# A row recurrence on one core: the order of the instructions in its loop written anew

## The chip, the cores and the metric

The kernel runs on one core of a Trainium2 chip. The metric is the time of one execution on the device, in microseconds (us), as the median of several executions. Five engines of the core take part, each with its own instruction stream that it works through strictly in order: PE (TensorE, matrix products; its weight loads are shown apart as PEld), ACT (ScalarE), DVE (VectorE), POOL (GpSimd) and SP (SyncE, which here only issues transfers). Across engines, an instruction waits on semaphores for the results that it needs.

## The reference

The input `x` holds 8 images of 96 channels and 128 rows of 128 pixels, in float32. It is normalised in 32 groups of channels; a masked convolution along the row gives four gates for every pixel; and then the rows are run through one after the other, as an LSTM whose hidden state `h` is itself convolved along the row (three taps):

```
its = conv(groupnorm(x), W_is * mask) + b_is          # 1x3, along a row
def step((h, c), row_in):                             # one row of all images
    gates = conv1d(h, W_ss, 3 taps) + b_ss + row_in
    f, i, o = sigmoid(three of the gates);  g = tanh(the fourth)
    c_new = f * c + i * g
    h_new = o * tanh(c_new)
out = x + all h_new
```

Row r + 1 can't start before `h` of row r is there. So 128 rows follow each other.

## The kernel before

**Half-steps.** The 8 images are cut into two halves of 4, which know nothing of each other. A half-step `n` is one row of one half: row `n // 2`, half `n % 2`. There are 256. While one half's gates go through the pointwise work, TensorE has the other half's products. Rows are loaded in blocks of four, by transfers that SP issues.

**Even and odd pixels.** A row is held as even and odd pixels apart, and the three taps are worked out from sums and differences of neighbours. From `h` of a half, VectorE makes the operand `vs` (the sum, `total`, L600), then `vf` (the difference, `difference`, L604), and GpSimd makes `vd` (`shifted`, L608). The first products of the half's next row need `vs`, the following `vf`, later ones `vd`. In the text that follows, "vs" at L600 is the operand on which the next row of that half hangs.

**The pointwise chain of a half-step.** ScalarE copies one half of a bank (`cpA`, `cpB`, `cpC`, L526); VectorE makes the even and the odd pixels' gates from it (`lo`, L530, and `hi`, L534); ScalarE takes tanh (`ta`, L538) and sigmoid (`si`, L550). Then, for the even pixels (`a`) and the odd ones (`b`) apart:

- the gated product i * g: `gtb` on VectorE (L564), `gta` on GpSimd (L562);
- the new cell: `ceb`, then `cea`, on VectorE (L574), which add f * c (`fg`, L555);
- tanh of the cell on ScalarE: `thb`, `tha` (L579);
- `h`: `oub`, `oua` on VectorE (L587), and straight behind them `vs` (L600) and `vf` (L604).

Behind them VectorE adds `h` to the row of `x` that goes out (`re`, L621, an instruction with both inputs in SBUF).

**GpSimd's other work.** Besides `vd` and `gta` GpSimd prepares the input of a later block of rows, spread over the half-steps. For one image of four rows, in three parts: `W1` normalises the own pixels into the buffer `xw` (L297, `xw<-xr`), `W2` adds neighbours (`add_pixels`, L314, `xs<-xw`, 256 elements in each of 128 partitions), `W3` subtracts them (`subtract_pixels`, L318, 512 elements). And it normalises channels that are shared (`U`, L297, `hx<-x`, in 32 partitions). In three half-steps of four that is one instruction of 512 or 384 elements; in those that follow the first row of a block it is two, one of 512 and a small one of 128 elements. The two halves take the first row one behind the other, so in every eight half-steps there are two such, which I call the heavy ones. GpSimd's first instruction behind the residual addition, `W1`, is held until that addition is done, and `vd` until `vf` is.

**What sets the order.** All four engines' streams are written by hand. The string `PERIOD` (L717) is read once for each half-step: each word is one or two instructions; a mark behind it says of which half-step (`'` the one before, `+` the next, `*` the one after that). Each engine's stream is the sequence of its own words in it. `prepare` (L680) issues the words `W1` to `W3` and `U`.

Of the kernel before, what the change touches and what calls it, by code (L numbers as in the profile page):

```python
# [21 lines left out]
def kernel(  # L22
# [32 lines left out]
    nc = tc.nc  # L55
# [354 lines left out]
    def hold(made, until):  # L410
        if until.ins.engine != E.Pool:
            tc.add_manual_dep(
                made.ins,
                until.ins.name,
                mybir.DependencyInfo(
                    mybir.DependencyClass.Sync, mybir.DependencyReason.SCHED_ONLY
                ),
                reason="GpSimd starts when VectorE is done with both SBUF reads",
            )
# [5 lines left out]
    class HalfStep:  # L425
# [141 lines left out]
        def part(self, ap, lo, hi, t=None):  # L567
            ap = ap.rearrange("p (t b j) -> p t b j", t=2, b=BH)
            return ap[:, :, lo:hi] if t is None else ap[:, t, lo:hi]
# [95 lines left out]
    def work(n):  # L665
        if n < len(FIRST):
            return FIRST[n]
        row, s = divmod(n, NH)
        k, r = divmod(row, R)
        ahead, image = (k + 2, 0) if r == R - 1 else (k + 1, r + 1)  # L670
        return (
            shared(s, k + 1, *SHARED[r]) if k + 1 < NB else [],
            own(s, ahead, image) if ahead < NB else (),
            ([(load_rows, s, k + 2)] if r == R - 2 and k + 2 < NB else [])
            + ([LATER[n]] if n in LATER else []),
        )
# [3 lines left out]
    def prepare(n, which="123"):  # L680

        channels, image, rest = worked.setdefault(n, [list(parts) for parts in work(n)])
        now = []
        for name, engine in (("X", nc.scalar), ("U", nc.gpsimd)):
            if name in which:
                now += [part for part in channels if part[1] is engine]
                channels[:] = [part for part in channels if part[1] is not engine]
        for i in "123":
            if i in which and int(i) <= len(image) and image[int(i) - 1]:
                now.append(image[int(i) - 1])  # L690
                image[int(i) - 1] = None
        if image.count(None) == len(image) and n not in closed:
            closed.add(n)
            now += rest
        for part, *args in now:
            made = part(*args)
            if made is not None and made.ins.engine == E.Pool and residuals:
                hold(made, residuals[-1])
                residuals.clear()
# [3 lines left out]
    def finish(n):  # L703
        prepare(n)
        row, s = divmod(n, NH)
        k, r = divmod(row, R)
        if r == R - 1:
            store(s, k, R - 1 if k + 1 == NB else 0, R)
            if k + 2 < NB:
                load(s, k + 2)  # L710
        elif r == R - 2 and k + 1 == NB:
            store(s, k, 0, R - 1)
# [2 lines left out]


    PERIOD = (  # L717
        "1A hiC' D'' X siBb' 1B 2A siBa' 2B 0C' siA' 2A re'' 3C' taB' 1A 1B fg' W1 0C' 2B cpA 3C' "
        "2C loA cpB U W2 EC' 1C loB PB+ PA+ taCa' hiA 1C taCb' QA+ hiB gta' 2C siC' gtb' 3A 3B EA "
        "ceb' cpC EB cea' 0A thb' W3 loC 0B tha' PC+ oub' 0A oua' 3B 3A S' 0B QB* F' taA QC+"  # L720
    )
    PIXELS = {"a": (0, BH, 0), "b": (0, BH, 1)}
    SPLIT = ("taC", "siB", "gt", "ce", "th", "ou")
# [8 lines left out]
    def half_step(n):  # L732
        if n not in steps:
            steps[n] = HalfStep(n)
        return steps[n]

    def do(n, names, by_lanes=False):

        for name in names.split():
            if name in "UX":  # L740
                if n >= NH:
                    prepare(n - NH, name)
                continue
            if name[0] == "W":
                prepare(n - 1 + name.count("+") - name.count("'"), name.strip("W+'"))
                continue
            at = n
            for mark, offset in (("'", -1), ("+", 1), ("*", 2)):
                at += offset * name.count(mark)
                name = name.replace(mark, "")  # L750
            pixels = PIXELS[name[-1]] if name[:-1] in SPLIT and name[-1] in PIXELS else ()
            whole_name = name[:-1] if pixels else name
            tile_ = whole_name[-1] if whole_name[-1] in order else ""
            part = whole_name[: len(whole_name) - len(tile_)]

            if part in ("S", "F", "D"):
                at += NH
            if not 0 <= at <= last:
                continue
            step = half_step(at)  # L760
            if name in step.done or whole_name in step.done:
                continue
            if by_lanes and (part in OWN or part in H_PRODUCTS) and (
                at < last or part in ("P", "Q") or (part, order[tile_]) in step.halves
            ):
                if step.piece(part, order[tile_]):
                    step.done.add(name)
                continue
            step.done.add(name)
            getattr(step, PARTS[part])(*([order[tile_]] if tile_ else []), *pixels)  # L770
            if by_lanes and part == "re":
                finish(at)
# [44 lines left out]
    def begin():  # L817
        operands(0)
        do(0, "PA PB QA QB PC QC 1A 2A 1B 2B 1C 2C")
# [7 lines left out]
    def next_products():  # L827


        late[0:0] = [Scale(1, 0, BH - 1)]  # L830
        late.insert(1, Scale(1, BH - 1, BH, late[0].banks))
        for a in range(3):
            half_step(1).take_bank(a)
        do(2, "PA PB QA QB PC QC 1A 2A 1B 2B 1C 2C")
# [18 lines left out]
    def keep_warm(count):  # L853
# [13 lines left out]
        at(4, 13): lambda: shared_rows(nc.scalar, 0, 0, R),  # L867
        at(5, 8): begin,
        at(5, 9): lambda: do(0, "cpA cpB cpC"),
        at(5, 17): lambda: do(  # L870
            0, "loA hiA EA 0A 3A loB hiB EB 0B 3B loC hiC EC 0C 3C taA taB siB taC siC"
# [174 lines left out]
```

## Time and profile before

| what | value |
|---|---|
| time of three executions | 2034.54 to 2035.09 us, median 2034.84 us |
| the profiled execution, first to last instruction | 2036.7 us |
| mean clock granted to TensorE | 0.997 of full speed |
| busy: PE, PEld, DVE, ACT, POOL | 95%, 91%, 89%, 76%, 65% of the span |

The profiled execution's own time is given as its span; it lies 1.9 us, or 0.1%, over the median of the runs. Busy time of PE isn't the time that it is at its peak: its products are pipelined and run in two row groups of 64 side by side, and an instruction is drawn until its modelled end.

The profile names instructions by engine, line and tiles, as `POOL xs<-xw L314`. In the timeline a row has the start, the time that it lasted, the engine, the line, and in brackets the idle time just before it and what ended that. Where "x2" stands, two like instructions in a row are drawn as one, from the start of the first to the end of the second.

### The profile page before, as it was taken

What the parts mean: (1) busy time and instruction counts of PE and PEld (TensorE: products, weight loads), DVE (VectorE), ACT (ScalarE), POOL (GpSimd) and SP (SyncE); (2) the same over time, 40 slices, a digit from 0 to 9 for tenths busy, and PEclk for the clock granted to TensorE, in tenths of its full rate; (3) what the DMA queues carried; (4) which work ended last, traced back from release to release, by engine and by line L of the source; (5) the groups of instructions that cost most, each with busy time, mean ns of one, the idle gap of its engine ahead of it and who ended that gap; (6) DMA issues with size and microseconds to landing.
All of it is one profiled execution on the core that took longest, in us unless ns stands there. A gap on an engine that the chain in (4) does not pass through costs nothing.

```text
span 2036.7 us, 45537 instructions
## 1 busy us (share of the span) xinstructions
PE 1935.3 (95%) x16936; PEld 1847.4 (91%) x16936; DVE 1812.6 (89%) x3997; ACT 1555.9 (76%) x3417; POOL 1329.7 (65%) x1708
## 2 busy tenths in 40 slices
PE   0389999999999999999999999999999999999998
PEld 0279999999999999999999999999999999999997
DVE  5768999999999999999999999999999999999998
ACT  4777777777777777777777777777777777777776
POOL 3347766666666666667666666666666666676651
PEclk9989999999999999999999999999999999999999
DMA  9994343344333334433433443333344333434411
GB/s 381 423 313 115 75 107 94 94 115 115 94 79 100 94 94 115 115 94 79 99 95 93 115 115 97 79 97 102 89 113 115 100 83 90 106 90 106 115 32 32
DMA packets 103388, 237.16 MB, mean 116 GB/s; under 512 B 5952, under 2 KB 8896, under 8 KB 97280
## 3 DMA queue, kind: packets, MB, share of 16 engines
q1 hardware_dynamic: 103168, 234.25, 42.0%
q8 instruction: 135, 2.21, 0.5%
q14 instruction: 85, 0.70, 0.1%
HBM read 183.90 MB, written 50.33 MB: 115 GB/s over the span
## 4 chain that ended last, share of the span: by engine, by line
PE 82%; DVE 7%; POOL 5%; DMA 4%; issue 1%; ACT 1%; SPq 0%; POOLq 0%; DVEq 0%; ACTq 0%
PE ps L460 82%; DMA xs<-in_x_dram 4%; DVE x L621 2%; POOL hx L297 2%; POOL xw L297 1%; DVE bst L919 1%; POOL xs L314 1%; DVE hx L587 1%; POOL g L562 1%; DVE vs L600 1%; DVE c L574 1%; DVE ps L530 1%; DVE ps L534 1%; DVE vf L604 1%; PE ps L174 0%
## 5 line engine op out<-in xcount | busy, mean ns | idle before, releaser
L460 PE MATMUL ps<-vd,wl 64*128 64x256 f32 (+1 forms) x6096 | 1275.6, 381 | 0.8 <-DVE ps L534 0.2
L460 PEld LDWEIGHTS ps<-vd,wl 64*128 64x128 f32 (+1 forms) x6096 | 943.4, 186 | 29.9 <-issue 1.7
L460 PE MATMUL ps<-vf,wm 64*128 64x256 f32 (+1 forms) x3052 | 752.7, 381 | 0.2
L460 PE MATMUL ps<-vs,wm 64*128 64x256 f32 (+1 forms) x3052 | 703.3, 384 | 5.9 <-POOL vs L600 4.0
L538 ACT ACTIVATE g<-ps 32x256 f32<-32x256 f32 (+1 forms) x1021 | 468.5, 481 | 301.0 <-PE ps L460 294.4
L460 PE MATMUL ps<-xs,wx 64*128 64x256 f32 x3080 | 676.8, 377 | 11.1 <-POOL xs L314 11.1
L460 PEld LDWEIGHTS ps<-vf,wm 64*128 64x128 f32 (+1 forms) x3052 | 504.7, 186 | 13.5 <-issue 0.8
L460 PEld LDWEIGHTS ps<-xs,wx 64*128 64x128 f32 x3080 | 491.8, 187 | 18.9 <-POOL xs L314 11.6
L608 POOL TENSOR_TENSOR vd<-hx 128x512 f32<-128x512 f32 x257 | 266.7, 1038 | 351.2 <-DVE vf L604 343.0
L460 PEld LDWEIGHTS ps<-vs,wm 64*128 64x128 f32 (+1 forms) x3052 | 432.4, 187 | 38.2 <-DVE vs L600 24.2
L530 DVE TENSOR_TENSOR ps<-m,ps 128x256 f32<-128x256 f32 x768 | 325.8, 425 | 98.7 <-ACT m L526 81.7
L526 ACT ACTIVATE m<-ps,wl 128x256 f32<-128x256 f32 x766 | 360.7, 474 | 56.6 <-PE ps L460 32.2
L550 ACT ACTIVATE ps<-ps 96x512 f32<-96x512 f32 x767 | 388.7, 507 | 14.4
L460 PE MATMUL ps<-xs,wt 64*128 64x256 f32 x1530 | 384.6, 377 | 0.0
L621 DVE TENSOR_TENSOR x<-x,hx 96x512 f32<-96x512 f32 x254 | 371.1, 1461 | 0.0
L297 POOL TENSOR_SCALAR xw<-xr,rstd,nmr 128x512 f32<-128x512 f32 x252 | 205.8, 817 | 181.9 <-DVE x L621 174.9
L534 DVE TENSOR_TENSOR ps<-m,ps 128x256 f32<-128x256 f32 x768 | 301.1, 422 | 1.3 <-PE ps L460 1.2
L318 POOL TENSOR_TENSOR xs<-xw 128x512 f32<-128x512 f32 (+1 forms) x254 | 270.0, 1063 | 0.0
L460 PEld LDWEIGHTS ps<-xs,wt 64*128 64x128 f32 x1530 | 264.8, 187 | 1.5 <-issue 1.0
L574 DVE TENSOR_TENSOR c<-ps,g 96x256 f32<-96x256 f32 x508 | 207.1, 419 | 55.3 <-POOL g L562 36.0
L297 POOL TENSOR_SCALAR hx<-x,rstd,nmr 32x512 f32<-32x512 f32 (+2 forms) x309 | 222.8, 721 | 32.6 <-DVE x L621 2.2
L579 ACT ACTIVATE th<-c 96x256 f32<-96x256 f32 (+1 forms) x510 | 203.7, 412 | 49.7 <-DVE c L574 37.9
(93 smaller groups left out, 1408.7 us busy)
## 6 DMA issues: line engine op xcount, KB each, us to landing
xr<-in_x_dram SPq DMA_DIRECT2D x124, 512.0 KB, 6.4
x<-in_x_dram SPq DMA_DIRECT2D x63, 768.0 KB, 6.0
out_dram<-x SPq DMA_DIRECT2D x62, 768.0 KB, 4.5
xs<-in_x_dram SPq DMA_DIRECT2D x30, 1024.0 KB, 12.3
piece<-in_x_dram SPq DMA_DIRECT2D x16, 1024.0 KB, 12.3
x<-in_x_dram SPq DMA_DIRECT2D x62, 256.0 KB, 3.2
xs<-in_x_dram SPq DMA_DIRECT2D x4, 512.0 KB, 8.3
out_dram<-x SPq DMA_DIRECT2D x2, 576.0 KB, 3.7
```

The costliest lines, as they stand in the source:

```text
L297: return engine.tensor_scalar(dst, src, scale, shift, ALU.mult, ALU.add)
L318: nc.gpsimd.tensor_sub(differences, strided(xw[:, 0, :], 0, [(W + 1, n), (J, 2), (1, J)]), strided(xw[:, 0, :], J + 1, [(W + 1, n), (0, 2) ...
L460: made = nc.tensor.matmul(self.ps[a][:, bass.ts(half, HB)][:, cols], weights[rows, bass.ts(a, P)], rhs[rows, cols], start=new, stop=False, ...
L526: nc.scalar.activation(self.m1[a], m1, AF.Identity, bias=column)
L530: nc.vector.tensor_add(self.ps[a][:, 0:HB], self.m1[a], self.ps[a][:, HB:])
L534: nc.vector.tensor_sub(hi, self.m1[a], hi)
L538: nc.scalar.activation(self.part(g, lo, hi, t), self.part(ps, lo, hi, t), AF.Tanh)
L550: nc.scalar.activation(to, gate, AF.Sigmoid)
L574: nc.vector.tensor_add(c, f, g)
L579: nc.scalar.activation(self.part(self.th, lo, hi, t), self.part(self.c, lo, hi, t), AF.Tanh)
L608: diff = nc.gpsimd.tensor_sub(self.operand("vd", 2)[:, :, lo:hi], strided(h, 1, [(BH * JP - 1, 2), (JP, hi - lo), (1, J)]), strided(h, 0, ...
L621: residuals.append(nc.vector.tensor_add(xo, xo, self.h))
```

## The change

The string `PERIOD` is written anew, `prepare` issues at most one part for each of `X`, `U` and a new word `V`, and `do` knows the word `V`:

```diff
-        for name, engine in (("X", nc.scalar), ("U", nc.gpsimd)):
+        for name, engine in (("X", nc.scalar), ("U", nc.gpsimd), ("V", nc.gpsimd)):
             if name in which:
-                now += [part for part in channels if part[1] is engine]
-                channels[:] = [part for part in channels if part[1] is not engine]
+                now += [part for part in channels if part[1] is engine][:1]
+                channels[:] = [part for part in channels if part not in now]
...
     PERIOD = (
-        "1A hiC' D'' X siBb' 1B 2A siBa' 2B 0C' siA' 2A re'' 3C' taB' 1A 1B fg' W1 0C' 2B cpA 3C' "
-        "2C loA cpB U W2 EC' 1C loB PB+ PA+ taCa' hiA 1C taCb' QA+ hiB gta' 2C siC' gtb' 3A 3B EA "
-        "ceb' cpC EB cea' 0A thb' W3 loC 0B tha' PC+ oub' 0A oua' 3B 3A S' 0B QB* F' taA QC+"
+        "1A hiC' D'' X siBb' 1B 2A siBa' 2B siA' 0C' 2A re'' 3C' taB' 1A 1B fg' W1 0C' 2B cpA "
+        "cpB 3C' 2C loA U V EC' 1C taCa' loB PB+ PA+ hiA 1C taCb' QA+ hiB gta' W3 2C siC' gtb' "
+        "3A 3B EA ceb' cpC cea' thb' EB 0A loC 0B tha' PC+ oub' 0A oua' 3B 3A 0B QB* S' F' taA "
+        "W2 QC+"
     )
...
-            if name in "UX":
+            if name in "UVX":
```

In the string many words move against each other, but most of them past words of other engines, which no engine sees. Read engine by engine, the streams of PE, ACT, DVE and SP hold the same instructions in the same sequence before and after; a single product on PE early in the row loop has one wait on GpSimd more. Only GpSimd's stream is another.

GpSimd's rows from one `vd` to the next, in an ordinary half-step (lines with a minus are of before, with a plus of after; the numbers behind a name tell buffers apart):

```order
 L608 TENSOR_TENSOR vd_10_2282<-hx_69 128x512
 L297 TENSOR_SCALAR xw_80<-xr_78,rstd_104,nmr_106 128x4x2x64
 L297 TENSOR_SCALAR hx_70<-x_3_1946,rstd_103,nmr_105 32x4x2x64
-L314 TENSOR_TENSOR xs_76<-xw_80 128x4x64
-L562 TENSOR_TENSOR g_9_2277<-i_9_2287,g_9_2277 96x256
-L318 TENSOR_TENSOR xs_76<-xw_80 128x4x2x64
+L562 TENSOR_TENSOR g_9_2276<-i_9_2287,g_9_2276 96x256
+L318 TENSOR_TENSOR xs_76<-xw_80 128x4x2x64
+L314 TENSOR_TENSOR xs_76<-xw_80 128x4x64
 L608 TENSOR_TENSOR vd_10_2367<-hx_71 128x512
```

The addition W2 (L314) has moved from ahead of the gated product `gta` (L562) to behind the subtraction W3 (L318), where it is the last ahead of the next `vd`.

The same in a heavy half-step, with its two normalisations of shared channels (L297, 512 and 128 elements):

```order
 L608 TENSOR_TENSOR vd_9_2110<-hx_69 128x512
 L297 TENSOR_SCALAR xw_80<-xr_78,rstd_104,nmr_106 128x4x2x64
 L297 TENSOR_SCALAR hx_70<-x_3_1946,rstd_103,nmr_105 32x4x2x64
 L297 TENSOR_SCALAR hx_70<-x_3_1946,rstd_103,nmr_105 32x2x64
-L314 TENSOR_TENSOR xs_76<-xw_80 128x4x64
-L562 TENSOR_TENSOR g_8_2105<-i_8_2115,g_8_2105 96x256
-L318 TENSOR_TENSOR xs_76<-xw_80 128x4x2x64
+L562 TENSOR_TENSOR g_8_2104<-i_8_2115,g_8_2104 96x256
+L318 TENSOR_TENSOR xs_76<-xw_80 128x4x2x64
+L314 TENSOR_TENSOR xs_76<-xw_80 128x4x64
 L608 TENSOR_TENSOR vd_9_2196<-hx_71 128x512
```

Again only W2 has moved; the small normalisation, which the new word `V` now issues, stays where it was, since `U` and `V` stand side by side.

In the last block of rows no image is left to prepare; there GpSimd's stream is the same before and after.

## The prediction

> **What bounds the kernel now.** The page first: busy time by engine, and the chain that ended last.
>
> ```profile
> PE 1935.3 (95%) x16936; PEld 1847.4 (91%) x16936; DVE 1812.6 (89%) x3997; ACT 1555.9 (76%) x3417; POOL 1329.7 (65%) x1708
> PE 82%; DVE 7%; POOL 5%; DMA 4%; issue 1%; ACT 1%; SPq 0%; POOLq 0%; DVEq 0%; ACTq 0%
> ```
>
> PE carries the chain, so a gain can only come from time in which PE has nothing to do. How much is that? Each half-step has one `vd` on GpSimd (L608), so the distance between their starts is the length of a half-step. From GpSimd's timeline, eight half-steps in the middle and six starts near the end:
>
> ```profile
> 1013.01 1.04 POOL L608 TENSOR_TENSOR vd<-hx 128x512 f32<-128x512 f32 x1 [1.36 <-DVE vf L604]
> 1034.62 1.04 POOL L608 TENSOR_TENSOR vd<-hx 128x512 f32<-128x512 f32 x1 [1.50 <-DVE vf L604]
> 1042.46 1.04 POOL L608 TENSOR_TENSOR vd<-hx 128x512 f32<-128x512 f32 x1 [1.36 <-DVE vf L604]
> 1050.31 1.04 POOL L608 TENSOR_TENSOR vd<-hx 128x512 f32<-128x512 f32 x1 [1.36 <-DVE vf L604]
> 1072.18 1.04 POOL L608 TENSOR_TENSOR vd<-hx 128x512 f32<-128x512 f32 x1 [1.36 <-DVE vf L604]
> ...
> 1974.60 1.04 POOL L608 TENSOR_TENSOR vd<-hx 128x512 f32<-128x512 f32 x1 [2.72 <-PE ps L460]
> ...
> 2010.75 1.04 POOL L608 TENSOR_TENSOR vd<-hx 128x512 f32<-128x512 f32 x1 [2.66 <-DVE vf L604]
> ```
>
> Eight half-steps take 1072.18 - 1013.01 = 59.17 us. Five in the last block, where GpSimd has next to nothing beside `vd` and `gta`, take 36.15, or 7.23 each: I take this as what PE needs. Three in the middle with all of GpSimd's work (1013.01 to 1034.62) take 7.20 each, so that floor isn't a gift of the quiet end. The two from 1034.62 to 1050.31 take 7.84 and 7.85. These are the heavy ones, and they hold 1.23 of the 59.17 - 8 x 7.23 = 1.33 us that eight half-steps lose. The waits name the place:
>
> ```profile
> POOL vd L608 <- DVE vf L604: 343.0, 248, 2.7
> DVE c L574 <- POOL g L562: 36.0, 63, 0.7
> ACT th L579 <- DVE c L574: 37.9, 67, 1.1
> PEld ps L460 <- DVE vs L600: 24.2, 63, 0.8
> ```
>
> Columns: us in total, times, longest. Read from below: 63 times PE waits for `vs`; some 63 times tanh of the cell waits for the cell, and the cell (`cea`) for GpSimd's `gta`. One chain, 63 times, which is the heavy half-steps:
>
> ```profile
> L297 POOL TENSOR_SCALAR hx<-x,rstd,nmr 32x128 f32<-32x128 f32 x60 | 27.5, 458 | 6.0
> ```
>
> The small normalisation runs 60 times: 30 groups of eight half-steps. `vd`'s long wait costs nothing, GpSimd is done by then.
>
> **W2 behind `gta`, heavy half-step.** GpSimd's and VectorE's rows of the second heavy one:
>
> ```profile
> 1045.14 1.37 POOL L297 TENSOR_SCALAR hx<-x,rstd,nmr 32x512 f32<-32x512 f32 x2
> 1046.59 0.64 POOL L314 TENSOR_TENSOR xs<-xw 128x256 f32<-128x256 f32 x1
> 1047.19 0.72 POOL L562 TENSOR_TENSOR g<-i,g 96x256 f32<-96x256 f32 x1
> 1047.88 1.07 POOL L318 TENSOR_TENSOR xs<-xw 128x512 f32<-128x512 f32 x1
> ...
> 1046.88 0.42 DVE L574 TENSOR_TENSOR c<-ps,g 96x256 f32<-96x256 f32 x1
> 1047.95 0.42 DVE L574 TENSOR_TENSOR c<-ps,g 96x256 f32<-96x256 f32 x1 [0.65 <-POOL g L562]
> 1049.40 0.43 DVE L600 TENSOR_TENSOR vs<-hx 128x256 f32<-128x256 f32 x1
> ```
>
> GpSimd is free of the normalisations at 1046.51. Its `gta` then starts between 1046.47 (it starts 0.04 ahead of the end of the addition now) and 1046.59 (where the addition starts now), and ends at 1047.19 to 1047.31. `cea` starts 0.04 behind that end now, so then at 1047.23 to 1047.35, which is 0.60 to 0.72 earlier. `ceb` doesn't hold it up: it starts at 1046.88, and two such instructions follow each other at 0.33 (below), so 1047.21. `vs` stands 1.45 behind `cea`, so it starts at 1048.68 to 1048.80, and the half-step of 7.85 could take 7.13 to 7.25: at PE's 7.23, within 0.02.
>
> **W2 behind `gta`, ordinary half-step.** Here ScalarE's tanh (`taCa`, first of the two) bounds `gta`:
>
> ```profile
> 1008.40 0.81 POOL L297 TENSOR_SCALAR hx<-x,rstd,nmr 32x512 f32<-32x512 f32 x1
> 1009.30 0.64 POOL L314 TENSOR_TENSOR xs<-xw 128x256 f32<-128x256 f32 x1
> 1009.90 0.72 POOL L562 TENSOR_TENSOR g<-i,g 96x256 f32<-96x256 f32 x1
> ...
> 1008.93 0.65 ACT L538 ACTIVATE g<-ps 32x256 f32<-32x256 f32 x2 [0.28 <-PE ps L460]
> L538 ACT ACTIVATE g<-ps 32x256 f32<-32x256 f32 x506 | 163.5, 369 | 72.3 <-PE ps L460 72.2
> 1010.13 0.95 DVE L574 TENSOR_TENSOR c<-ps,g 96x256 f32<-96x256 f32 x2
> 1011.33 0.74 DVE L587 TENSOR_TENSOR hx<-ps,th 96x256 f32<-96x256 f32 x2
> 1012.11 0.43 DVE L600 TENSOR_TENSOR vs<-hx 128x256 f32<-128x256 f32 x1
> ```
>
> The pair of L587 takes 0.74, of which one is 0.41, so the second starts 0.33 behind the first. The pair of L574 takes 0.95: `cea` starts at 1010.66, 0.53 behind `ceb`, because `gta` ends at 1010.62. One tanh takes 0.37 (the last row, a group), so `taCa` ends at 1009.30; `gta` from there ends at 1010.02, and `cea` can start 0.33 behind `ceb`, at 1010.46. So `vs` comes 0.20 earlier, at 1011.91. Ordinary half-steps lose little now ((1.33 - 1.23) / 6 = 0.02 on the mean, 0.07 in one of 7.30), so most of this isn't gain but a margin, about 0.13, by which `vs` is there ahead of PE.
>
> **What W2 meets in its new place.** It reads and writes SBUF on GpSimd just when VectorE turns to `vs`, both of whose inputs are in SBUF. Early in the row loop there are three such meetings:
>
> ```profile
> 166.10 0.82 POOL L297 TENSOR_SCALAR xw<-xr,rstd,nmr 128x512 f32<-128x512 f32 x1
> 211.65 0.82 POOL L297 TENSOR_SCALAR xw<-xr,rstd,nmr 128x512 f32<-128x512 f32 x1
> 240.54 2.09 POOL L318 TENSOR_TENSOR xs<-xw 128x512 f32<-128x512 f32 x2
> ...
> 166.72 0.47 DVE L600 TENSOR_TENSOR vs<-hx 128x256 f32<-128x256 f32 x1
> 212.12 0.62 DVE L600 TENSOR_TENSOR vs<-hx 128x256 f32<-128x256 f32 x1
> 242.07 0.84 DVE L600 TENSOR_TENSOR vs<-hx 128x256 f32<-128x256 f32 x1
> ```
>
> GpSimd's instruction ended 0.20, 0.35 and 0.56 behind the start of `vs`, which took 0.04, 0.19 and 0.41 over its 0.43: the price is the overlap less 0.15. In the heavy half-step W3 starts 0.03 ahead of the end of `gta`, as now, or up to 0.08 behind it if its wait on its own engine costs that (0.08 is the gap between normalisation and addition now). It takes 1.07, and W2 follows 0.03 ahead of its end and takes 0.64. So W2 ends 1.65 to 1.76 behind the end of `gta`, and `vs` starts 1.49 behind it: overlap 0.16 to 0.27, price 0.01 to 0.12. If PE and not `gta` sets the pace, the overlap is smaller. The first heavy half-step of a pair hides that in the margin of 0.13; the second may come up to 0.15 late. For 30 pairs, 0 to 4.5 us. I take 1.0, near the lower end, since the middle overlap of 0.21 costs 0.06, less than the margin. In the ordinary half-step W2 ends at 1010.02 + 1.65 to 1.76 = 1011.67 to 1011.78, ahead of `vs` at 1011.91: free.
>
> The Trainium skill has this under SBUF — State Buffer, section SBUF: two separate sides: VectorE with two SBUF inputs and GpSimd share a port pair by an exclusive lock, and the loser blocks for the whole instruction. The three rows agree that `vs` isn't merely slowed but ends behind GpSimd's instruction; taken as a block of the whole overlap, the page's rule is the second rival below.
>
> **The rest of the diff.** `vd`, next on GpSimd behind W2, comes at 1013.01 and waits 1.36 for `vf` now; that idle time takes the 0.1 or so that the sequence may grow. The sums that W2 writes are read by products of a later half-step, at least one whole half-step on. The row loads that follow the last of W1 to W3 keep their place in SP's stream. `U` and `V` stand together, the copies keep their place on ScalarE: nothing. Three of the 63 waits lie outside the 30 groups, at about 0.6 each.
>
> **Sum.** 30 x 1.33 = 39.9, and 3 x 0.6 = 1.8, less 1.0 for the meetings: 40.7 us. The profiled execution's 2036.7 becomes 1996.0. It stands 1.9 over the median of the runs, so 1994.1.
>
> **Rivals.**
>
> *PE's floor isn't quite reached, or is lower.* With 7.20 for 7.23, 30 x 0.24 = 7 us more would go, which the meetings then take back in part: 1990 as the lower end. With all 4.5 of the meetings: 1997.6. I count 1990 to 1998 to the forecast: 0.72.
>
> *The meetings cost more.* If `vs` loses its whole overlap of 0.16 to 0.27, that is 60 x 0.16 to 0.27 less 30 x 0.13 of margin, 6 to 12 us: 1999 to 2005. If W3 or W2 also slips and the overlap is 0.5, with 0.35 lost each time, 17 us: 2010. For it speaks that the end of W2 and the start of `vs` lie so near each other; against it the three rows, in which 0.15 was free each time. 0.19, between 1998 and 2012.
>
> *Slower.* W2 meets `vs` in every half-step. If `gta` waited so long that W2 started only as `vs` does, `vs` would lose 0.64 - 0.15 = 0.49, less 0.13, in some 241 half-steps: +87 us over the forecast, 2081. It decides from an overlap of about 0.45 (0.17 us of gain a half-step, 0.13 of margin, 0.15 free), so W2 would have to end 0.6 later than reckoned. Nothing in the rows does that: 0.04.
>
> *No change.* `cea` is free and something else holds `vs` where it is, say `tha` behind ScalarE's copy. Since `vs` kept its 1.45 behind `cea` in both kinds of half-step (1049.40 - 1047.95, 1012.11 - 1010.66), whatever `cea` waited: 0.03, around 2034. 0.02 stays for what I don't see, on either side.
>
> **Chances.** Faster by over 0.2% (4 us, about what a measurement of this kernel can tell): 0.93; within 0.2%: 0.03; slower: 0.04. The range reaches from 1990 into the second case, to 2004.
>
> **What would show it.** `vd` starts 7.23 apart in heavy half-steps too; the wait of the cell for GpSimd's `g` (63 times) gone or under 0.1 each; PE's wait for `vs` down from 24.2 to under 5 us; `vs` at 0.43 to 0.55 in heavy half-steps and 0.43 in ordinary ones. I am wrong if `vs` lasts 0.6 or more, if the half-step with `vs` on time is still over 7.3, or if `gta` finds another wait.

## The result, and the profile after

| kernel | time, median | lowest to highest | against before, 95% interval |
|---|---|---|---|
| before | 2034.92 us | 2034.54 to 2035.09 (4 runs) | |
| after | 1999.45 us | 1998.61 to 2000.09 (4 runs) | 0.9826 [0.9812, 0.984] |

The change makes the kernel 1.7% faster: 35.5 us, where 40.7 were forecast. The time is inside the range, 5.4 us over the predicted 1994.1; it lies past 1998, where the forecast's main case ended. The profiled execution of after spans 1998.2 us and took 1999.95, so a device time lies about 1.75 us over its span (1.7 to 1.9 in every run).

Busy time by engine, and the shares of the chain that ended last, of after:

```profile
PE 1897.3 (95%) x16936; PEld 1840.1 (92%) x16936; DVE 1804.1 (90%) x3997; ACT 1535.8 (77%) x3417; POOL 1326.3 (66%) x1708
PE 92%; DMA 4%; DVE 1%; ACT 1%; POOL 0%; issue 0%; SPq 0%; DVEq 0%; POOLq 0%; ACTq 0%
```

The busy shares say nearly nothing: PE stands at 95% before and after. In the first profile of before, PE had 82% of the chain, and DVE and POOL 12% together: in most groups of eight half-steps the chain left PE once, for 8.2 us. Now the longest of the chain's pieces is the row loop in one:

```profile
180.92 1801.04 PE ps L460 x16386
```

Those are start, length and what: 1801 us in which the chain follows nothing but products. This alone proves little: a second profile of before, below, has its chain on PE as well, and its loop is as slow as in the first but for 0.2%. What tells the two kernels apart are the waits (us in total, times, longest):

```profile
POOL vd L608 <- DVE vf L604: 133.7, 139, 1.1
POOL g L562 <- ACT g L538: 93.6, 191, 5.2
ACT th L579 <- DVE c L574: 2.2, 6, 1.1
PEld ps L460 <- DVE vs L600: 1.9, 5, 0.7
DVE c L574 <- POOL g L562: 0.6, 2, 0.4
```

The chain of three waits that came 63 times is down to a handful, nearly all at the loop's ends: the cell's for `gta` from 36.0 to 0.6 us, PE's for `vs` from 24.2 to 1.9. Instead `gta` now waits 191 times for ScalarE's tanh. That is not a new stall: GpSimd has less to do ahead of it and so is early.

A heavy half-step of after, GpSimd's rows and below them VectorE's:

```profile
1024.57 1.04 POOL L608 TENSOR_TENSOR vd<-hx 128x512 f32<-128x512 f32 x1 [0.77 <-PE ps L460]
1027.24 1.37 POOL L297 TENSOR_SCALAR hx<-x,rstd,nmr 32x512 f32<-32x512 f32 x2
1028.69 0.72 POOL L562 TENSOR_TENSOR g<-i,g 96x256 f32<-96x256 f32 x1
1029.38 1.06 POOL L318 TENSOR_TENSOR xs<-xw 128x512 f32<-128x512 f32 x1
1030.40 0.63 POOL L314 TENSOR_TENSOR xs<-xw 128x256 f32<-128x256 f32 x1
1031.81 1.04 POOL L608 TENSOR_TENSOR vd<-hx 128x512 f32<-128x512 f32 x1 [0.77 <-DVE vf L604]
...
1029.12 0.75 DVE L574 TENSOR_TENSOR c<-ps,g 96x256 f32<-96x256 f32 x2
1030.90 0.43 DVE L600 TENSOR_TENSOR vs<-hx 128x256 f32<-128x256 f32 x1
```

`vd` to `vd` is 7.24, about as long as the others (7.16 to 7.30 on the mean, by place in the eight). `gta` starts 0.08 behind the normalisations, and the two cells run as one pair of 0.75, so nothing separates them now. W2 ends at 1031.03, 0.13 behind the start of `vs`, and `vs` lasts 0.43, its undisturbed time: the overlap is just within the 0.15 that had cost nothing in the rows of before.

Over the loop, the `vd` 224 half-steps apart (28 groups of eight), of before and then of after:

```profile
243.39 1.04 POOL L608 TENSOR_TENSOR vd<-hx 128x512 f32<-128x512 f32 x1 [0.76 <-DVE vf L604]
1901.04 1.04 POOL L608 TENSOR_TENSOR vd<-hx 128x512 f32<-128x512 f32 x1 [1.36 <-DVE vf L604]
```

```profile
243.54 1.04 POOL L608 TENSOR_TENSOR vd<-hx 128x512 f32<-128x512 f32 x1 [0.76 <-DVE vf L604]
1863.76 1.04 POOL L608 TENSOR_TENSOR vd<-hx 128x512 f32<-128x512 f32 x1 [1.07 <-DVE vf L604]
```

1657.65 us became 1620.22: 59.20 and 57.87 for eight half-steps, 7.400 and 7.233 for one. The forecast's floor was 7.23. I call the time for eight half-steps, taken so, the pace.

### The profile page after: what moved, and what is told of

It reads as the page before. It is cut to its first block, busy times and chain, and to the rows that moved or that the text cites. A ratio compares the mean times of both kernels' runs of the same rounds, so it can differ in the third digit from the quotient of the medians.

```text
span 1998.2 us, 45596 instructions
## 1 busy us (share of the span) xinstructions
PE 1897.3 (95%) x16936; PEld 1840.1 (92%) x16936; DVE 1804.1 (90%) x3997; ACT 1535.8 (77%) x3417; POOL 1326.3 (66%) x1708
## 4 chain that ended last, share of the span: by engine, by line
PE 92%; DMA 4%; DVE 1%; ACT 1%; POOL 0%; issue 0%; SPq 0%; DVEq 0%; POOLq 0%; ACTq 0%
PE ps L460 92%; DMA xs<-in_x_dram 4%; DVE bst L920 1%; ACT g L538 0%; ACT xs L216 0%; ACT xs L217 0%; POOL xw L297 0%; POOL xs L314 0%; POOL xs L318 0%; ACT piece L295 0%; SPq L908 0%; ACT ps L550 0%; DVE hx L587 0%; DVE st L826 0%; ACT th L579 0%
## 5 line engine op out<-in xcount | busy, mean ns | idle before, releaser
L460 PE MATMUL ps<-vs,wm 64*128 64x256 f32 (+1 forms) x3052 | 715.2, 378 | 4.6 <-POOL vs L600 4.0
L460 PEld LDWEIGHTS ps<-vf,wm 64*128 64x128 f32 (+1 forms) x3052 | 528.3, 187 | 10.7 <-issue 0.8
L460 PEld LDWEIGHTS ps<-vs,wm 64*128 64x128 f32 (+1 forms) x3052 | 468.9, 187 | 16.7 <-POOL vs L600 5.1
L526 ACT ACTIVATE m<-ps,wl 128x256 f32<-128x256 f32 x766 | 355.4, 473 | 22.9 <-PE ps L460 5.0
L297 POOL TENSOR_SCALAR xw<-xr,rstd,nmr 128x512 f32<-128x512 f32 x252 | 204.6, 812 | 181.6 <-DVE x L621 174.7
L318 POOL TENSOR_TENSOR xs<-xw 128x512 f32<-128x512 f32 (+1 forms) x254 | 269.4, 1061 | 0.1
L562 POOL TENSOR_TENSOR g<-i,g 96x256 f32<-96x256 f32 x252 | 182.8, 725 | 98.4 <-ACT g L538 93.6
L297 POOL TENSOR_SCALAR hx<-x,rstd,nmr 32x512 f32<-32x512 f32 (+2 forms) x309 | 222.1, 719 | 32.6 <-DVE x L621 2.2
L574 DVE TENSOR_TENSOR c<-ps,g 96x256 f32<-96x256 f32 x508 | 191.4, 416 | 9.2 <-POOL g L562 0.6
```

The lines of the kernel that those rows point to most:

```text
L297: return engine.tensor_scalar(dst, src, scale, shift, ALU.mult, ALU.add)
L318: nc.gpsimd.tensor_sub(differences, strided(xw[:, 0, :], 0, [(W + 1, n), (J, 2), (1, J)]), strided(xw[:, 0, :], J + 1, [(W + 1, n), (0, 2) ...
L460: made = nc.tensor.matmul(self.ps[a][:, bass.ts(half, HB)][:, cols], weights[rows, bass.ts(a, P)], rhs[rows, cols], start=new, stop=False, ...
L526: nc.scalar.activation(self.m1[a], m1, AF.Identity, bias=column)
L562: nc.gpsimd.tensor_mul(to, i, g)
L574: nc.vector.tensor_add(c, f, g)
```

## The experiments

The theory was that W2's place ahead of `gta` is the whole cause: `gta` and all behind it is late in the heavy half-steps, and with W2 behind it PE sets the pace everywhere. The rivals: another of the rewritten words did it; meetings of W2 with `vs` take part of the gain back; and, for the 5 us that were missed, something ahead of the loop or the loop's own pace. The kernels ran in two batches. In the first, before took 2035.49 us (median of 19 runs), in the second, on another chip, 2038.04 (7 runs).

**Before once more, for its pace.** No edit.

> The kernel before once more, for its own profile. My sum was made against a profiled execution of 2036.7 us from first to last instruction, and set against a median time of 2034.8; yet of the changed kernel each time lies 1.75 us over its span. If the span is always 1.75 below the time, the profile of before was of an execution 3.5 us longer than the usual one, and this run should show a span near 2033 with the row loop at 59.17 us for eight half-steps as there, so that the 3.5 us lie ahead of the loop. The rival is that the loop itself runs at another pace in other executions (59.05 for eight would do): then the gain of the loop is smaller than the two profiles say.

Measured: 2035.41 us, ratio 1.0001 [0.9991, 1.001]. The profiled execution took 2035.97 at a span of 2034.2, so 1.77 over it. The same two `vd`:

```profile
243.62 1.04 POOL L608 TENSOR_TENSOR vd<-hx 128x512 f32<-128x512 f32 x1 [0.76 <-DVE vf L604]
1898.55 1.04 POOL L608 TENSOR_TENSOR vd<-hx 128x512 f32<-128x512 f32 x1 [1.36 <-DVE vf L604]
```

1654.93 us, or 59.10 for eight. So the same program ran its loop at another pace in another execution: 2.7 us over 28 groups, where the two spans differ by 2.5. The stretch ahead of the loop isn't it. Whether it is the execution or the chip stays open, since it isn't known on which chip the first profile was taken; but single executions far from the median occur within this batch too (2038.68 the slowest of the 19). The chain of this profile:

```profile
PE 92%; DMA 4%; ACT 2%; DVE 1%; issue 0%; POOL 0%; SPq 0%; POOLq 0%; DVEq 0%; ACTq 0%
```

It is the chain of after, all but the same, in a kernel that is 1.8% slower, and the waits are those of before: 60 of the cell for `gta`, 63 of PE for `vs`. So the share of PE in the chain doesn't show whether PE sets the pace; the waits and the distance of the `vd` do.

**Only W2, in the text of before.**

```diff
-        "2C loA cpB U W2 EC' 1C loB PB+ PA+ taCa' hiA 1C taCb' QA+ hiB gta' 2C siC' gtb' 3A 3B EA "
-        "ceb' cpC EB cea' 0A thb' W3 loC 0B tha' PC+ oub' 0A oua' 3B 3A S' 0B QB* F' taA QC+"
+        "2C loA cpB U EC' 1C loB PB+ PA+ taCa' hiA 1C taCb' QA+ hiB gta' 2C siC' gtb' 3A 3B EA "
+        "ceb' cpC EB cea' 0A thb' W3 loC 0B tha' PC+ oub' 0A oua' 3B 3A S' 0B QB* F' taA W2 QC+"
```

> The text of before, with W2 alone moved to the end of the string; words U, V and X, the copies and the S' and F' as before. Theory (all of the gain is W2 behind the gated product): the time of the changed kernel, 1998 to 2001. Rival (the other moved words matter for what the engines do): at least a fifth of the gain is missing, 2007 or more.

Measured: 1999.57 us, ratio 0.9823 [0.9808, 0.9837], against 0.9826 of the whole change.

**The change without it.** The text of after, with W2 put back.

```diff
-        "cpB 3C' 2C loA U V EC' 1C taCa' loB PB+ PA+ hiA 1C taCb' QA+ hiB gta' W3 2C siC' gtb' "
+        "cpB 3C' 2C loA U V W2 EC' 1C taCa' loB PB+ PA+ hiA 1C taCb' QA+ hiB gta' W3 2C siC' gtb' "
...
-        "W2 QC+"
+        "QC+"
```

> The changed text, with W2 alone put back ahead of the gated product, behind U and V. Theory: the time of before, 2033 to 2036, with 63 waits of the cell for GpSimd's gated product. Rival (other words matter): 2028 or less.

Measured: 2035.74 us, ratio 1.0003 [0.9993, 1.0012]. The waits, first of W2 alone moved, then of W2 put back:

```profile
PEld ps L460 <- DVE vs L600: 1.9, 5, 0.7
DVE c L574 <- POOL g L562: 0.6, 2, 0.4
```

```profile
DVE c L574 <- POOL g L562: 34.6, 60, 0.7
PEld ps L460 <- DVE vs L600: 23.1, 63, 0.7
```

One word carries all of it in both directions, and the waits go and come with it. The rest of the rewritten string, the word `V` and the limit of one part each are worth nothing that the runs can tell.

**A second addition behind W2.** To price the meetings, GpSimd adds once more from `xw` to a spare tile in the heavy half-steps alone, straight behind W2; nothing reads that tile.

```diff
-        "W2 QC+"
+        "W2 Z QC+"
...
+            if name == "Z":
+                if n >= 10 and (n - NH) // NH % R == 0 and (n - NH) // NH // R + 1 < NB:
+                    nc.gpsimd.tensor_add(spare[:, 0:256].rearrange("p (r j) -> p r j", r=R), xw[0][:, 0:R, 0:J], xw[0][:, 0:R, J + 1 :])
+                continue
```

> The changed kernel, with one more addition of W2's size (0.64 us, xw into a spare tile that nobody reads) behind W2 in the heavy half-steps alone. It ends 0.75 us behind the start of vs. Theory (vs waits for the end of GpSimd's instruction, less 0.15 us that are free; margin 0.13): vs lasts 1.03 in the heavy half-steps, PE loses 0.60 + 0.60 - 0.13 us in each of some 30 pairs: 32 us, 2031. Rival 1 (both are only slowed, in shares): vs at 0.5 to 0.6, at most 6 us, 1999 to 2006. Rival 2 (vs isn't what PE waits for once the gated product is on time): vs at 1.03 and the time still 1999 to 2001.

Measured: 2019.48 us, ratio 0.9922 [0.9907, 0.9936], 20 us over W2 moved alone and short of the 2031 expected. A heavy half-step, GpSimd and then VectorE:

```profile
447.48 0.64 POOL L314 TENSOR_TENSOR xs<-xw 128x256 f32<-128x256 f32 x1
448.08 0.82 POOL L744 TENSOR_TENSOR spare<-xw 128x256 f32<-128x256 f32 x1
...
447.98 0.43 DVE L600 TENSOR_TENSOR vs<-hx 128x256 f32<-128x256 f32 x1
448.32 0.86 DVE L604 TENSOR_TENSOR vf<-hx 128x256 f32<-128x256 f32 x1
```

I had expected `vs` to wait for both additions. It got in as W2 ended, 0.14 behind its start, and lasted 0.43. Then the second addition was the one held up (0.82 for 0.64), and `vf`, which has both inputs in SBUF too, waited for that (0.86 for about 0.42). So in these rows the two engines take turns, instruction by instruction: what comes first holds, and the other goes next. The price was real but fell one instruction later. From 57.87 the pace rose to 58.53; 0.66 x 29 groups is 19 of the 20 us.

**The same place, written only.** A memset of the spare tile, about as long as that addition, which reads nothing.

```diff
-                    nc.gpsimd.tensor_add(spare[:, 0:256].rearrange("p (r j) -> p r j", r=R), xw[0][:, 0:R, 0:J], xw[0][:, 0:R, J + 1 :])
+                    nc.gpsimd.memset(spare, 0.0)
```

> The changed kernel, with a fill of a spare tile by zeros (about 0.64 us, it writes SBUF and reads none) behind W2 in the heavy half-steps alone, where the run before had an addition of the same length, in which vf took 0.86 instead of 0.42 and the time was 2019.5. Theory (VectorE and GpSimd share the way by which operands are read): vf stays at 0.42, the time at 1999 to 2001. Rival (any instruction of GpSimd at that place keeps vf waiting, by the place and not by its reads): vf at 0.86 and 2019.

Measured: 1999.12 us, ratio 0.9807 [0.9793, 0.9822] on the second chip: nothing lost that shows against the 1999.45 of after, which itself wasn't run in this batch.

```profile
444.45 0.64 POOL L314 TENSOR_TENSOR xs<-xw 128x256 f32<-128x256 f32 x1
445.04 0.62 POOL L744 MEMSET spare<- 128x640 f32 x1
...
444.94 0.43 DVE L600 TENSOR_TENSOR vs<-hx 128x256 f32<-128x256 f32 x1
445.30 0.41 DVE L604 TENSOR_TENSOR vf<-hx 128x256 f32<-128x256 f32 x1
```

`vf` lies beside the memset from 445.30 to 445.66 and lasts 0.41. So it is GpSimd's reading that holds VectorE up, not that GpSimd is busy or writes. The Trainium skill says the same in SBUF — State Buffer, section Who interferes with whom: VectorE with two SBUF inputs contends with a GpSimd instruction that reads SBUF and not with one that only writes it, and "Issue order, not op shape, decides who blocks". The rows of these two runs agree with both, but for the 0.14 that `vs` lay beside W2 and lost nothing by.

**W2 later.** A memset of 0.31 us ahead of W2 in the heavy half-steps, so that W2 itself meets `vs`.

```diff
-        "W2 QC+"
+        "Z W2 QC+"
...
+                    nc.gpsimd.memset(spare[:, 0:256], 0.0)
```

> The changed kernel, with a short fill (about 0.3 us, writes alone) ahead of W2 in the heavy half-steps, so that W2 ends some 0.44 behind the start of vs instead of 0.14. Theory (of a meeting 0.15 is free, the rest is paid by vs, and 0.13 of that is hidden by the margin once a pair): vs at 0.72, PE loses 0.29 + 0.29 - 0.13 = 0.45 in each of 29 pairs: 13 us, 2012 to 2013. Rival 1 (vs gets through between two reads of GpSimd as it did in the run with the second addition): vs at 0.43 and 1999 to 2001. Rival 2 (the margin is larger than 0.13 in both half-steps of a pair): vs at 0.72 and less than 2005.

Measured: 2010.49 us, ratio 0.9863 [0.9847, 0.988]: 11.4 us over the memset behind W2, on the same chip.

```profile
445.26 0.31 POOL L744 MEMSET spare<- 128x256 f32 x1
445.53 0.64 POOL L314 TENSOR_TENSOR xs<-xw 128x256 f32<-128x256 f32 x1
...
445.77 0.68 DVE L600 TENSOR_TENSOR vs<-hx 128x256 f32<-128x256 f32 x1
```

W2 ended 0.40 behind the start of `vs`, which lasted 0.25 over its 0.43. That is the forecast's price (the overlap less 0.15), on the operand on which PE hangs: the two heavy half-steps of this stretch took 14.99 together, where with the memset behind W2 they took 14.51, and the half-step after them won 0.06 back. A pace of 58.23 against 57.85, 0.38 in each of 29 groups, gives 11.0. The forecast's rival of a dearer meeting was a real danger, then: 0.27 us more of overlap took back nearly a third of the gain.

**`gta` ahead of the shared normalisations too.** If `gta` early is good, is earlier better?

```diff
-        "cpB 3C' 2C loA U V EC' 1C taCa' loB PB+ PA+ hiA 1C taCb' QA+ hiB gta' W3 2C siC' gtb' "
+        "cpB 3C' 2C loA EC' 1C taCa' loB PB+ PA+ hiA 1C taCb' QA+ hiB gta' U V W3 2C siC' gtb' "
```

> The changed kernel with the gated product still further ahead on GpSimd, in front of the normalisations U and V. Theory: it then stands waiting for ScalarE's tanh with U, V, W3 and W2 queued behind it. GpSimd is free 2.6 us behind vd, tanh is over at 3.8, so the rest shifts by about 1.0 us; W3 and W2 then run while VectorE makes vs and vf in every half-step, vs or vf is 0.4 or more late each time, against a margin of 0.13: 0.3 us in some 230 ordinary half-steps and more in the heavy ones, 2065 to 2100, slower than before. Rival (what counts is that nothing stands in front of the gated product): 2000 or less.

Measured: 2108.22 us, ratio 1.0342 [1.0327, 1.0358], a little beyond the slow end expected. Two `vd` eight half-steps apart, an ordinary half-step between them, and the wait of `gta`:

```profile
983.41 1.04 POOL L608 TENSOR_TENSOR vd<-hx 128x512 f32<-128x512 f32 x1 [0.43 <-DVE vf L604]
1044.92 1.04 POOL L608 TENSOR_TENSOR vd<-hx 128x512 f32<-128x512 f32 x1 [0.43 <-DVE vf L604]
...
1002.03 0.72 POOL L562 TENSOR_TENSOR g<-i,g 96x256 f32<-96x256 f32 x1 [1.07 <-ACT g L538]
1004.66 0.83 POOL L314 TENSOR_TENSOR xs<-xw 128x256 f32<-128x256 f32 x1
...
1004.90 0.86 DVE L604 TENSOR_TENSOR vf<-hx 128x256 f32<-128x256 f32 x1
```

```profile
POOL g L562 <- ACT g L538: 275.0, 252, 5.2
```

`gta` now stands at the head of GpSimd's queue and waits about 1 us for tanh in every half-step, with the normalisations, W3 and W2 behind it. So W3 ends while `vs` runs (0.55 on the median and 1.1 in the heavy half-steps, for 0.43; in the half-step shown the overlap is 0.14, and `vs` loses nothing), and W2 falls between `vs` and `vf`, which lasts 0.86 in every half-step. The pace is 61.51, and 3.64 x 29 = 106 us of the 109 over after. This is close to the forecast's rival for slower, a W2 that meets VectorE in every half-step (there put at 2081).

**Another product ahead of the wait.** With PE at its floor, can PE be filled better? `QA+`, the next row's own-pixel products, was put later, behind `PC+`, to fill two short gaps that PE was thought to have there.

```diff
-        "cpB 3C' 2C loA U V EC' 1C taCa' loB PB+ PA+ hiA 1C taCb' QA+ hiB gta' W3 2C siC' gtb' "
-        "3A 3B EA ceb' cpC cea' thb' EB 0A loC 0B tha' PC+ oub' 0A oua' 3B 3A 0B QB* S' F' taA "
+        "cpB 3C' 2C loA U V EC' 1C taCa' loB PB+ PA+ hiA 1C taCb' hiB gta' W3 2C siC' gtb' "
+        "3A 3B EA ceb' cpC cea' thb' EB 0A loC 0B tha' PC+ QA+ oub' 0A oua' 3B 3A 0B QB* S' F' taA "
```

> The changed kernel with one product (QA of the next half-step) moved on PE from behind 1C to behind PC, between the two visits to the banks of 3A, 3B, 0A and 0B. In the changed kernel PE's half-step of 7.23 holds two gaps of 0.11 us at that place, where a product waits for the other row group's products in its bank. Theory (the gap is the length of that wait, and one more product between fills it; the time that PE gains is then bounded by vs, which is 0.13 early): half-steps of 7.10 to 7.13, 1970 to 1977. Rival 1 (the gap goes to where QA stood): 1999 to 2001 or more. Rival 2 (the pointwise chain is as long as PE's work already): no change, with waits for vs in each half-step.

Measured: 2153.16 us, ratio 1.0562 [1.0546, 1.0578]: a plain miss.

```profile
1000.46 1.04 POOL L608 TENSOR_TENSOR vd<-hx 128x512 f32<-128x512 f32 x1 [1.11 <-DVE vf L604]
1008.50 1.04 POOL L608 TENSOR_TENSOR vd<-hx 128x512 f32<-128x512 f32 x1 [1.01 <-DVE vf L604]
1016.09 1.04 POOL L608 TENSOR_TENSOR vd<-hx 128x512 f32<-128x512 f32 x1 [1.05 <-DVE vf L604]
```

```profile
PEld ps L460 <- issue: 70.8, 140, 0.7
```

Half-steps of 8.04 and 7.59, and next to no wait for `vs` (1.1 us in all). PE lost the time in itself: waits put down to "issue" are 70.8 us where after has 5.1, which is 66 of the 154 us over after. The kernel gives its products to the two row groups in turn, so a moved product turns round the groups of those behind it, and the code makes a product wait whose bank was last written by the other group. This is read from the code; no run took it apart, so the cause stays open. What it shows is only that this filling doesn't lower the 7.23.

## Why the prediction was right, and where it was off

**W2 behind `gta` is the cause: shown,** in both directions.

**Heavy half-steps come to PE's 7.23, and no lower: right.** 57.87 for eight measured, 57.84 forecast. In the row loop from its second group on (from the `vd` at 243 us to the last one), 29 groups were worth 38.67 us between the two profiles, and 29 x 1.33 is 38.6. The rival of a lower floor is out.

**The meetings in the heavy half-steps: mis-sized, at 1.0 us, measured 0.** Reckoned was an overlap of 0.16 to 0.27; the trace has 0.13, as W2 ends 1.62 behind the end of `gta` and not 1.65 or more. The price itself holds: W2 later gave 0.25 for an overlap of 0.40, and 0.40 - 0.15 = 0.25. From the second group on no `vs` of after is longer than 0.43, so ordinary half-steps are free too, as forecast. That the heavy ones are hangs on the 0.02 between 0.13 and 0.15, which the first profile couldn't promise.

**Taking the first group and the three extra waits as full gain: the first step that failed.** They were put at 1.33 + 1.8 = 3.1 us; the profiles give 0.70. Here GpSimd has instructions that the later half-steps don't have, and the forecast reckoned what W2 meets only for the steady heavy and ordinary half-steps. `vs` in six early half-steps, of after, with GpSimd's rows at the first; below, `vs` of before at the first:

```profile
158.53 1.32 DVE L600 TENSOR_TENSOR vs<-hx 128x256 f32<-128x256 f32 x1
167.34 0.65 DVE L600 TENSOR_TENSOR vs<-hx 128x256 f32<-128x256 f32 x1
175.26 0.45 DVE L600 TENSOR_TENSOR vs<-hx 128x256 f32<-128x256 f32 x1
183.24 0.87 DVE L600 TENSOR_TENSOR vs<-hx 128x256 f32<-128x256 f32 x1
227.31 0.71 DVE L600 TENSOR_TENSOR vs<-hx 128x256 f32<-128x256 f32 x1
241.93 1.13 DVE L600 TENSOR_TENSOR vs<-hx 128x256 f32<-128x256 f32 x1
...
158.51 1.06 POOL L318 TENSOR_TENSOR xs<-xw 128x512 f32<-128x512 f32 x1
159.53 0.82 POOL L314 TENSOR_TENSOR xs<-xw 128x256 f32<-128x256 f32 x1
```

```profile
157.92 0.91 DVE L600 TENSOR_TENSOR vs<-hx 128x256 f32<-128x256 f32 x1
```

The long W3 now comes ahead of the short W2, and so it is W3 on which the first `vs` falls: 1.32 in place of 0.91. That 0.91 of before is a fourth early meeting, where the forecast named three. Of the others, the second, fourth, fifth and sixth were 0.47, 0.43, 0.43 and 0.84 before. So saved waits turned into meetings. Between the fifth and the ninth `vd` (151.17 to 183.55 us before, 151.78 to 184.59 after) the change even costs: 32.81 us for 32.38. The first four lasted 1.31, 0.63, 0.45 and 0.87 with W2 alone moved, and that stretch 32.79, where with W2 put back it was 32.38; so this comes from W2's place and not from the word `V`. The longer `vs` add up to 1.6 of the 2.4 us that are missing here; the rest is not accounted for.

Between the two profiles the sum is thus 38.67 + 0.70, less 0.87 for a later start of the first products (a scatter ahead of the loop: in the ten traces they start anywhere from 89.8 to 92.1 us, the latest with W2 put back). That makes the 38.5 us by which the spans differ, where 40.7 was forecast: 2.2 of the miss.

**"It stands 1.9 over the median of the runs, so 1994.1": the second step that failed.** The forecast took the profiled execution's distance to the median as scatter that any kernel would share. It isn't. Two things lie in it. The time is 1.75 over the span, so that execution took about 2038.4, 3.5 us over the median. And most of the 3.5 is loop pace: 59.20 against the 59.10 of the second profile of before, 2.7 us. At 59.10 there is less to save, while with W2 behind `gta` the pace hardly moves (57.85 to 57.87 in after, with W2 alone moved and with the memset). So 1.9 was subtracted from a kernel that doesn't have it, and 1.75 between span and time was left out. With the 2.2 that makes 5.85 us; after's profiled execution was 0.5 over its own median, which leaves the 5.35 missed.

In other words, the first profile showed a slower before than the median runs are; the second profile, at 59.10, took 2035.97 and stands 0.6 from its median.

**The range: right by its width.** 1999.45 lies outside the 1990 to 1998 of the main case (0.72), in the stretch that was given to dearer meetings (0.19). In the steady loop the meetings cost nothing; what brought the time there are the two steps above, and early in the loop, in part, meetings that the forecast hadn't reckoned. The mechanism was right, but the case in which the time fell isn't the one that was argued for.

**`gta` behind tanh, `vd`, the copies, `U` with `V`: right,** at nothing. `gta`'s 191 waits for tanh cost the path nothing, since PE's wait for `vs` is gone all the same.

## What to carry to other kernels

Where two engines share a stall, count whose work stands ahead of the late instruction in its queue, and move the one piece that nobody waits for; then look at what that piece meets in its new place, in the loop's first rounds as much as in its steady state. Move it far enough to be out of the way and no farther: here 0.3 us later cost nearly a third of the gain, and moving the waiting instruction to the head of its queue cost three times the gain. A forecast made from one profile should give the saving at that profile's own pace, and ask how far that profile lies from the median run before it carries the distance over to another kernel. And a chain that lies on one engine isn't yet a proof that this engine sets the pace: here it lay on PE in a kernel that waited 60 times for GpSimd.

## What the runs showed of the hardware that was not expected

**GpSimd's normalisations weren't equally long in each profile.** Those by groups (total and mean in ns behind the bar) in the first profile of before, and in the second:

```profile
L297 POOL TENSOR_SCALAR xw<-xr,rstd,nmr 128x512 f32<-128x512 f32 x252 | 205.8, 817 | 181.9 <-DVE x L621 174.9 <-DVE nmr L289 6.5
```

```profile
L297 POOL TENSOR_SCALAR xw<-xr,rstd,nmr 128x512 f32<-128x512 f32 x252 | 204.1, 810 | 182.3 <-DVE x L621 175.4 <-DVE nmr L289 6.5
```

0.9% apart; the other normalisation (814 and 809) and W2 (643 and 640) differ likewise, the gated product (725 in both) doesn't. The four traces of the first batch have 808 to 812 for the row shown, the four of the second, on the other chip, 813 to 820, and before is 2.5 us slower on that chip. So it may be the chip, the execution or what the instruction meets; no run took that apart. Nor is it shown that the loop's pace hangs on it. Three such differences make 15 ns in a half-step, or 0.12 in eight, about the 0.10 by which the paces differ; but only the heavy half-steps hang on GpSimd's queue, and of the 0.10 they hold 0.04. What the runs do show is that the changed order doesn't follow: the memset behind W2 ran with 815 at 57.85.

**VectorE and GpSimd take turns.** A VectorE instruction with two SBUF inputs that is held up goes in between two GpSimd instructions that stand straight behind each other, and then the second of these waits (0.82 for 0.64, with a second addition behind W2). An overlap of up to 0.14 cost `vs` nothing; beyond 0.15 it ended about 0.28 behind GpSimd's instruction (0.68 long at an overlap of 0.40, 1.32 at 1.04).
